# Layer 1's stacks in DRAM: each pair's 2 KB with a gap of 16 bytes behind it

## The chip, the core and the metric

The kernel runs on one core of a Trainium2 chip. The metric is the device time of one execution in microseconds (us). It is given as the median of several runs, and as the time of one execution that the hardware profiler recorded. The core's engines are TensorE (PE), VectorE (DVE), ScalarE (ACT), GpSimd (POOL) and SyncE (SP). SP does no arithmetic here: it issues nearly all of the DMA transfers, one after the other, and waits before each for what the transfer needs.

## The reference

The model is a decoder of two layers over x of 32 sequences x 128 tokens x 128 channels. Layer 0 has an RWKV block, two attentions with feed-forward, and a mixture of experts. Layer 1 has a self-attention with rotary positions, a cross-attention with SiLU in place of softmax, and a mixture of experts with capacity. A layer norm follows each. The change concerns the scores of layer 1's two attentions:

```python
# _L1_attn_ref: 16 heads of 8 channels
q = _rope(split_heads(x @ Wq + bq)); k = _rope(split_heads(x @ Wk + bk))
scores = jnp.einsum('bhqd,bhkd->bhqk', q, k) / np.sqrt(D_K)
probs = jax.nn.softmax(scores, axis=-1)
# _L1_xattn_ref: 16 heads of 8 channels
scores = jnp.einsum('bhqd,bhkd->bhqk', q, k) * SCALE
attn = jax.nn.silu(jnp.where(mask == 0, NEG_INF, scores))
```

## The kernel before

The work is cut into 8 groups of 4 sequences (G = 4, GT = 512 tokens). Each layer's part of a group is a list of units, each with a place on a common time line. `pipeline` (L1467) sorts all of them by place and runs them in that order, so that several groups and layers are under way at once. The tile framework then fixes each engine's own order and sets the semaphores. A tile of SBUF comes from a ring of a few buffers (`BUFS`, L35): the stacks are of the kind `big`, with five buffers of 8 KB in each partition, shared with other work.

In layer 1 a head has only 8 channels, and q and k are kept to nearly single precision by splitting each into three bf16 parts (`parts3`, L801, on GpSimd). The score is the sum of six products of parts. The kernel does that sum in one matmul: it puts the six parts of q that are wanted, 8 rows each, on 48 partitions, and the six parts of k that go with them in the same partitions. Such an arrangement is a stack. As the parts lie on the wrong partitions for it (128 partitions: channel, parity of the head and number of the pair of heads), they go through DRAM:

- `scratch` (L810) makes three tensors `d_st` in DRAM, used in turn, of 64 rows x 2 parities x 8 pairs x 2 (q and k) x 512 tokens in bf16. One row, parity and pair has 2 KB, q and k beside each other; one row of both parities has 32 KB. Rows 48 to 63 are filled once from the input `pad_bf` (L816), near the start of the program.
- `spill` (L824) writes one group's parts. L829 writes the three parts to the rows 0 to 23, in pieces of 2 KB; L831 (once for q, once for k) the rows 24 to 39, in pieces of 1 KB; L832 the rows 40 to 47, in pieces of 1 KB. SP issues all four. They can start as the parts are done on GpSimd.
- `stack` (L835) reads half of the pairs back, once for each parity, into the partitions 0 to n and 64 to 64 + n (L843). Four consecutive pairs of one row are contiguous in DRAM: 8 KB. n is 50 in the self-attention, where rows 48 and 49 carry the maximum of the scores (written into the stack later, by `mwrite`, L1011, and `mread`, L1016, through the small DRAM tensor `d_m`), and 48 in the cross-attention. Each group has four reads in each attention, 64 in all.

`cross` (L979) and `probs` (L1130) run the matmuls on the stacks. On SP's queue the transfers around these are the loads and stores of x between layers (L217, L226), of the context (L580), of masks (L1117) and of expert weights (L1252); a transfer that has to wait holds all behind it.

Of the kernel before, what the change touches and what calls it, by code (L numbers as in the profile page):

```python
# [11 lines left out]
BF = mybir.dt.bfloat16  # L12
# [7 lines left out]

G = 4
GT = G * 128

# [47 lines left out]
class Net:  # L73
    def __init__(self, ctx, tc, a, ngroups):
# [15 lines left out]
        nc.gpsimd.tensor_copy(self.identb, self.ident)  # L90
        self.mhalf = self.cst.tile([128, G], F32, name="mhalf")
        nc.gpsimd.memset(self.mhalf, -0.5)
# [14 lines left out]
    def tok(self, tag):  # L107
        return self.t(tag, [G, 128])

# [93 lines left out]
    def half_turns(self, pts, es):  # L203

        calls = []
        for h in range(2):
            for b in range(G):
                for z in range(2):
                    r = slice(z * 64, z * 64 + 64)
                    calls.append((pts[z][:, (h * G + b) * 64:(h * G + b) * 64 + 64], es[h][r, b * 128:(b + 1) * 128],  # L210
                                  self.ident[r, r], None))
# [8 lines left out]
    def putx(self, g, x, final=False, queue=None):  # L220
        if final:
            d = self.a["out"][g * G:(g + 1) * G].rearrange("b s d -> s b d")
        else:
# [586 lines left out]
    def scratch(self, k):  # L810

        if self.dst is None:
            self.dst = []
            for i in range(3):
                d = self.dp.tile([64, 2, 8, 2, GT], BF, name=f"d_st{i}")
                self.nc.sync.dma_start(out=d[48:64], in_=self.a["pad_bf"])  # L816
                self.dst.append(d)
        return self.dst[k % 3]

# [4 lines left out]
    def spill(self, k, p):  # L824

        dma = self.nc.sync.dma_start
        d = self.scratch(k)
        rows = lambda lo, n: d[lo * 8:(lo + n) * 8].rearrange("(a d) r q z t -> (d r q) a z t", d=8)
        dma(out=rows(0, 3), in_=p)  # L829
        for z in range(2):  # L830
            dma(out=rows(3, 2)[:, :, z, :], in_=p[:, z:z + 2, z, :])  # L831
        dma(out=rows(5, 1)[:, 0], in_=p.rearrange("p a z t -> p (a z) t")[:, 0:6:5, :])  # L832
        return d

    def stack(self, d, h, n, slab=False):  # L835

        if slab:
            s = self.wp.tile([128, 4128], BF, name="w8", tag="w8", bufs=W8)
            s = s[:, 0:8 * GT].rearrange("p (q z t) -> p q z t", q=4, z=2)
        else:  # L840
            s = self.t("stack", [4, 2, GT], BF)
        for par in range(2):
            self.nc.sync.dma_start(out=s[par * 64:par * 64 + n], in_=d[0:n, par, h * 4:h * 4 + 4])  # L843
        return s

    def pad9(self):
# [92 lines left out]
    def att_units(self, g, getw, done):  # L939
# [129 lines left out]
        for j in range(8):  # L1069
            h = j // 4  # L1070
            u = [(L6["smax"], lambda j=j: smax(j)), (L6["probs"], lambda j=j: probs(j), 2),
                 (L6["values"], lambda j=j: values(j), 1)]
            if j == 0:
                u += [(0, load), (L6["pre"], pre), (L6["spill"], spill)]
                u += [(L6["v"] + 2 * b, lambda b=b: vproj(b)) for b in range(G)]
                for i in range(2):
                    u += [(L6["rope"] + 4 * i, lambda i=i: rope(i, 0)), (L6["rope"] + 2 + 4 * i, lambda i=i: rope(i, 1)),
                          (L6["part"] + 4 * i, lambda i=i: part(i))]
            if j % 4 == 0:
                u.append((L6["take"], lambda h=h: take(h)))  # L1080
            if j % 4 == 3:
                m = L6["mrow"]
                u += [(m, lambda h=h: mrow(h)), (m + 2, lambda h=h: mwrite(h)), (m + L6["mread"], lambda h=h: mread(h))]
            if h:
                u.append((L6["norm"], lambda b=j % 4: norm(b)))
            if j == 5:
                u += [(L6["norm"] - 2, again), (L6["norm"], bias)]
            if j == 7:
                o = L6["oproj"]
                u += [(o, oproj), (L6["done"], lambda: done(st["ln"](), nc.scalar))]  # L1090
            units.append([p if len(p) > 2 else (*p, -p[0]) for p in u])
# [13 lines left out]
    def xat_units(self, g, getw, done):  # L1105
# [103 lines left out]
        for j in range(8):  # L1209
            u = [(L7["probs"], lambda j=j: probs(j), 2), (L7["values"], lambda j=j: values(j), 1)]  # L1210
            if j == 0:
                u += [(0, load), (L7["pre"], pre), (L7["spill"], spill), (L7["mask"] - 2, mload), (L7["mask"], mask)]
                u += [(L7["v"] + b, lambda b=b: vproj(b)) for b in range(G)]
                for i in range(2):
                    u += [(L7["one"] + 2 * i, lambda i=i: one(i, *((st["kh"], st["kl"]) if i else (st["xh"], st["xl"])))),
                          (L7["part"] + 2 * i, lambda i=i: part(i))]
                u += [(t, lambda h=h: take(h)) for h, t in enumerate(L7["take"])]
            if j % 2:
                u.append((L7["oproj"], lambda b=j // 2: oproj(b)))
            if j == 7:  # L1220
                u += [(L7["ln"], lambda: st.update(y=st["ln"]())), (L7["done"], lambda: done(st["y"]))]
            units.append([p if len(p) > 2 else (*p, -p[0]) for p in u])
# [425 lines left out]
```

## Time and profile before

| | us |
|---|---|
| median of 3 runs (lowest, highest) | 1808.09 (1808.03, 1809.1) |
| the profiled execution | 1817.27 |
| its span, first to last instruction | 1815.5 |
| PE busy, share of the span | 1628.6, 90% |
| DVE busy | 1380.2, 76% |
| ACT busy | 1214.1, 67% |
| POOL busy | 982.6, 54% |
| stack reads L843, first and last issue | 1130.2, 1520.3 |

The granted clock of TensorE was 0.961 of full speed over the span. The page's slices are 40 equal parts of the span, some 45.4 us each; a digit is a busy share in tenths. "DMA" is the mean busy share of the core's 16 DMA engines. A DMA engine counts as busy while a packet of its own is under way, also if the packet waits somewhere. The chain of waits goes back from the last instruction, at each step to what released it. A wait of SP ("SPq") is time in which its queue stood still.

In the profile's list of transfers, each of the 32 reads of 50 rows moves 400 KB and each of the 32 reads of 48 rows 384 KB. A group's spill is three transfers of 256 KB and one of 768 KB. The three pad writes move 512 KB each.

### The profile page before, as it was taken

What the parts mean: (1) busy time and instruction counts of PE and PEld (TensorE: products, weight loads), DVE (VectorE), ACT (ScalarE), POOL (GpSimd) and SP (SyncE); (2) the same over time, 40 slices, a digit from 0 to 9 for tenths busy, and PEclk for the clock granted to TensorE, in tenths of its full rate; (3) what the DMA queues carried; (4) which work ended last, traced back from release to release, by engine and by line L of the source; (5) the groups of instructions that cost most, each with busy time, mean ns of one, the idle gap of its engine ahead of it and who ended that gap; (6) DMA issues with size and microseconds to landing.
All of it is one profiled execution on the core that took longest, in us unless ns stands there. A gap on an engine that the chain in (4) does not pass through costs nothing.

```text
span 1815.5 us, 45617 instructions
## 1 busy us (share of the span) xinstructions
PE 1628.6 (90%) x15858; PEld 1311.8 (72%) x15858; DVE 1380.2 (76%) x5303; ACT 1214.1 (67%) x3889; POOL 982.6 (54%) x1324
## 2 busy tenths in 40 slices
PE   4898898899999999998899999998877887989898
PEld 2676676777777777776688888876655554778898
DVE  7879888887777777775676667778864775788896
ACT  3786777878888888887744554336666666656654
POOL 4657676777665555564534444345533443446455
PEclk7899999999999999999999999999989998899999
DMA  6100110111110000000123443336667987223222
GB/s 172 36 26 23 41 44 24 33 48 56 49 39 9 27 25 26 27 25 14 58 79 124 167 154 109 108 124 196 182 184 173 246 231 204 93 71 105 82 94 70
DMA packets 86214, 163.43 MB, mean 90 GB/s; under 512 B 12968, under 2 KB 34352, under 8 KB 80368
## 3 DMA queue, kind: packets, MB, share of 16 engines
q1 hardware_dynamic: 83248, 146.89, 27.5%
q0 software_dynamic: 1584, 11.54, 1.5%
q8 instruction: 125, 2.05, 0.5%
q10 hardware_dynamic: 1152, 2.10, 0.3%
q14 instruction: 105, 0.86, 0.2%
HBM read 106.75 MB, written 55.31 MB: 89 GB/s over the span
## 4 chain that ended last, share of the span: by engine, by line
PE 41%; DVE 20%; ACT 15%; POOL 11%; issue 6%; DMA 6%; SPq 1%; POOLq 0%; ACTq 0%; DVEq 0%
ACT e L483 8%; PE mm L157 5%; PE S L771 5%; PE PV L169 4%; PE mm L158 4%; PE mm L159 4%; DVE e L478 4%; PE S L169 3%; POOL x L255 3%; PE mm L541 3%; PE PT L1395 3%; POOL e L487 2%; DMA x<-x 2%; DVE x L263 2%; PE S L620 1%
## 5 line engine op out<-in xcount | busy, mean ns | idle before, releaser
L483 ACT ACTIVATE e<-e,nm 128x128 f32<-128x128 f32 x1024 | 398.8, 394 | 111.8 <-POOL nm L480 111.8
L487 POOL TENSOR_TENSOR e<-e,ri 128x512 f32<-128x512 f32 x256 | 268.4, 1054 | 175.2 <-DVE ri L485 146.2
L478 DVE CUSTOM_DVE_ANT_0 e<-S,msk 128x128 f32<-128x128 f32 x1024 | 227.9, 284 | 12.0 <-PE PT L168 9.1
L483 ACT ACTIVATION_READ_ACCUMULATOR e<-e,nm 128x1 f32 x1024 | 196.2, 192 | 0.0
L169 PEld LDWEIGHTS S<-qk 64*128 64x128 f32 x2048 | 128.3, 190 | 78.0 <-issue 40.6
L169 PE MATMUL S<-qk 64*128 64x128 f32 x2048 | 151.3, 287 | 30.2 <-DVE pt L501 16.3
L169 PE MATMUL PV<-pt,v 128*64 128x128 f32 x2048 | 141.9, 281 | 10.8 <-DVE big L523 10.6
L157 PE MATMUL mm<-xs,w 128*128 128x512 f32 x296 | 130.9, 446 | 16.5 <-ACT xs L150 5.0
L276 POOL TENSOR_SCALAR rsqv<-bmv 128x4 f32<-128x4 f32 (+1 forms) x73 | 22.5, 308 | 215.3 <-DVE bmv L243 179.9
L771 PEld LDWEIGHTS S<-w,v 128*128 128x128 f32 x1024 | 129.1, 191 | 10.2 <-ACT v L760 1.9
L760 ACT ACTIVATE v<-mm,col_moe_b 128x512 f32<-128x512 f32 x128 | 85.6, 686 | 75.4 <-PE mm L159 74.8
L771 PE MATMUL S<-w,v 128*128 128x128 f32 x1024 | 133.9, 276 | 1.7 <-ACT v L760 1.7
L485 DVE RECIPROCAL ri<-su 128x4 f32<-128x4 f32 x256 | 43.6, 172 | 120.7 <-ACT e L483 90.7
L169 PEld LDWEIGHTS PV<-pt,v 128*64 128x64 f32 x2048 | 110.9, 138 | 21.6 <-issue 6.7
L158 PE MATMUL mm<-xs,w 128*128 128x512 f32 x296 | 119.8, 405 | 1.6 <-DVE xs L151 1.4
L159 PE MATMUL mm<-xs,w 128*128 128x512 f32 x296 | 119.1, 402 | 0.0
L169 PE MATMUL PV<-e,w 128*32 128x128 f32 (+1 forms) x2048 | 90.3, 299 | 26.3 <-ACT e L1027 13.9
L501 DVE COPY pt<-PT 128x256 f32<-128x256 f32 x256 | 97.3, 415 | 8.4 <-ACT pt L501 7.6
L523 DVE TENSOR_TENSOR big<-PV,big 128x512 fp32r<-128x512 f32 x128 | 87.3, 682 | 19.5 <-ACT big L522 19.0
L1000 DVE TENSOR_REDUCE amx<-mm 128x4 f32<-128x512 f32 x128 | 82.1, 684 | 24.3 <-PE mm L169 24.2
L501 ACT COPY pt<-PT 128x256 f32<-128x256 f32 x256 | 81.8, 373 | 25.2 <-PE PT L168 25.0
L541 PE MATMUL mm<-big 128*128 128x512 f32 x384 | 96.9, 398 | 0.0
(326 smaller groups left out, 4803.7 us busy)
## 6 DMA issues: line engine op xcount, KB each, us to landing
x<-x SPq DMA_DIRECT2D x151, 256.0 KB
pt<-d_w SPq DMA_DIRECT2D x64, 256.0 KB
big<-d_st SPq DMA_DIRECT2D x32, 400.0 KB
d_st<-qk SPq DMA_DIRECT2D x48, 256.0 KB
d_st<-qk SPq DMA_DIRECT2D x16, 768.0 KB
big<-d_st SPq DMA_DIRECT2D x32, 384.0 KB
d_w<-big POOLq DMA_DIRECT2D x11, 1024.0 KB, 6.4
w<-d_w SPq DMA_DIRECT2D x7, 1024.0 KB
```

The source lines that it names most:

```text
L157: mm(out=out, lhsT=wh, rhs=xh, start=True, stop=False)
L158: mm(out=out, lhsT=wh, rhs=xl, start=False, stop=False)
L159: mm(out=out, lhsT=wl, rhs=xh, start=False, stop=True)
L169: return self.nc.tensor.matmul(out=out, lhsT=lhsT, rhs=rhs, **more)
L478: self.seen = nc.vector.tensor_tensor_reduce(e[:, t], s[h][:, t], msk[:, t], 1.0, NEG, ALU.add, ALU.max, mx[:, b:b + 1])
L483: nc.scalar.activation(e[:, t], e[:, t], AF.Exp, bias=nm[:, b:b + 1], scale=0.125, accum_out=su[:, b:b + 1])
L487: i = nc.gpsimd.tensor_tensor(e3, e3, ri.unsqueeze(2).to_broadcast([128, G, 128]), ALU.mult)
L501: last = (nc.vector.tensor_copy if h else nc.scalar.copy)(d, s_)
L523: nc.vector.tensor_tensor(lo, o, hi.bitcast(F32), ALU.subtract)
L541: nc.tensor.matmul(out=out, lhsT=a_, rhs=b_, start=n == 0, stop=n == 3 * PER - 1)
L760: nc.scalar.activation(h, hp, AF.Gelu, bias=w["b1"][:, k:k + 1])
L771: nc.tensor.matmul(out=o[:, b, :], lhsT=hs[i][:, b * 128:(b + 1) * 128], rhs=w["w2"][:, k * 128:k * 128 + 128], start=i == 0, stop=i == 1)
```

## The change

`d_st` gets 16 bytes (GAP = 8 elements of bf16) behind each pair's 2 KB. A pair then takes 2,064 bytes and a row of 16 pairs 33,024. All that write or read it leave the gap out. What lay contiguous over several pairs is now a row of separate pieces: a stack read has four pieces of 2 KB for each row instead of one of 8 KB, and a pad write 256 pieces of 2 KB instead of 16 rows of 32 KB. The pieces of `spill` keep their sizes; their addresses in DRAM move. Inside SBUF nothing moves.

```diff
+GAP = 8
 G = 4
 GT = G * 128
...
-                d = self.dp.tile([64, 2, 8, 2, GT], BF, name=f"d_st{i}")
-                self.nc.sync.dma_start(out=d[48:64], in_=self.a["pad_bf"])
+                d = self.dp.tile([64, 2, 8, 2 * GT + GAP], BF, name=f"d_st{i}")
+                self.nc.sync.dma_start(out=d[48:64, :, :, 0:2 * GT], in_=self.a["pad_bf"].rearrange("p r q z t -> p r q (z t)"))
...
-        rows = lambda lo, n: d[lo * 8:(lo + n) * 8].rearrange("(a d) r q z t -> (d r q) a z t", d=8)
-        dma(out=rows(0, 3), in_=p)
+        rows = lambda lo, n: d[lo * 8:(lo + n) * 8].rearrange("(a d) r q x -> (d r q) a x", d=8)
+        dma(out=rows(0, 3)[:, :, 0:2 * GT], in_=p.rearrange("p a z t -> p a (z t)"))
         for z in range(2):
-            dma(out=rows(3, 2)[:, :, z, :], in_=p[:, z:z + 2, z, :])
-        dma(out=rows(5, 1)[:, 0], in_=p.rearrange("p a z t -> p (a z) t")[:, 0:6:5, :])
+            dma(out=rows(3, 2)[:, :, z * GT:(z + 1) * GT], in_=p[:, z:z + 2, z, :])
+        dma(out=rows(5, 1)[:, 0, 0:2 * GT].rearrange("p (z t) -> p z t", z=2), in_=p.rearrange("p a z t -> p (a z) t")[:, 0:6:5, :])
...
-            self.nc.sync.dma_start(out=s[par * 64:par * 64 + n], in_=d[0:n, par, h * 4:h * 4 + 4])
+            self.nc.sync.dma_start(out=s[par * 64:par * 64 + n].rearrange("p q z t -> p q (z t)"),
+                                   in_=d[0:n, par, h * 4:h * 4 + 4, 0:2 * GT])
```

## The prediction

> **What bounds the kernel now.** I read the page first, for the stages. Layer 1's two attentions, the only ones that use the stacks, lie between 1109 and 1565 us.
>
> ```profile
> PE   4898898899999999998899999998877887989898
> DMA  6100110111110000000123443336667987223222
> GB/s 172 36 26 23 41 44 24 33 48 56 49 39 9 27 25 26 27 25 14 58 79 124 167 154 109 108 124 196 182 184 173 246 231 204 93 71 105 82 94 70
> ```
>
> TensorE is the busiest engine in almost every slice. Only in slices 27 to 34 (1225 to 1565 us) do the DMA engines come near it, at six to nine tenths. The change can matter there, and at the start (the pad writes). Next, stretches in which one group's stacks are read with little beside them, and one spill:
>
> ```profile
> core 0: us, PE busy (x) PEld busy (x) DVE busy (x) ACT busy (x) POOL busy (x), PEclk, DMA share, GB/s
> 1127.20:1129.40 2.20, 2.20 (x19) 1.99 (x18) 0.00 (x0) 0.99 (x2) 0.00 (x0) 1.00 0.96 357
> 1131.00:1141.50 10.50, 10.50 (x74) 9.57 (x73) 10.11 (x47) 3.89 (x7) 2.42 (x26) 1.00 0.59 157
> 1439.90:1450.10 10.20, 7.97 (x114) 5.34 (x114) 7.96 (x23) 6.30 (x13) 8.49 (x9) 0.88 1.02 187
> ```
>
> The second last column is the busy share of the 16 DMA engines. The spill (first row) moves 357 GB/s with all engines. Four reads of 50 rows (second row) keep 0.59 x 16 = 9.4 engines busy and move 157, that is 16.6 GB/s for a busy engine instead of 23.2; four reads of 48 rows (third row) keep all 16 busy and move 187, other traffic included. So a stack read is slow while its engines count as busy. The packet records say the same: an 8 KB packet of other loads takes 309 ns, one of a 50-row read 489 on average (1131 to 1141 us), one of a 48-row read 720 (1440 to 1450 us). Packets of 2 KB take 84 ns nearly everywhere, 86 to 91 in spills; 1 KB 46, 512 B 27.
>
> Then the chain of waits over 1090 to 1570 us, its DMA pieces alone, and what holds SP:
>
> ```profile
> 1301.42 7.11 DMA d_m<-m
> 1309.16 2.89 DMA x<-x
> 1320.19 7.86 DMA big<-d_st
> 1365.82 6.35 DMA d_m<-m
> 1372.78 4.59 DMA big<-d_st
> 1391.76 6.26 DMA big<-d_st
> 1500.35 9.36 DMA x<-x
> 1530.85 2.57 DMA x<-x
> ```
>
> ```profile
> SPq L1019 <- DMA d_m<-m: 62.9, 15, 6.9
> SPq L843 <- DMA d_st<-qk: 49.7, 18, 8.0
> ```
>
> Start, length, what. Stack reads end the wait three times, for 7.86 + 4.59 + 6.26 = 18.7 us; small transfers queued behind stacks and spills on the same queue five times, for 28.3 us. Together 47 us of the path are DMA time that the change touches. Elsewhere in the 480 us the chain runs over TensorE, VectorE and ScalarE, and the reads are hidden under them: under TensorE busy all 10.50 us in the second row above, for example. L843 waits 49.7 us in total for its spill to land, and all later SP transfers wait behind it.
>
> **The change part by part.** In the built program, TensorE, VectorE, ScalarE and GpSimd have the same instructions in the same order, and SP the same transfers in the same order. Only shapes differ: L843 from 50x4096 to 50x4x1024 elements, L832 from 256x1x512 to 128x2x512, L816 from 16x16384 to 256x1024. No wait is added.
>
> *Reads (L843, 64 of them).* Each 8 KB piece becomes four of 2 KB, on the same engines and to the same partitions. From packets without contention: 4 x 84 = 336 against 309 ns, 27 more. A 50-row read puts 5 rows on each of 10 engines, a group of four reads 20 packets in a row: 20 x 27 = 0.54 us more. A 48-row group has 12 in a row on 16 engines: 0.32 us. These are upper bounds of about 5% (0.54 of 10.4) and 3%. The lower bound is nothing: where packets already wait 180 (489 - 309) or 411 ns (720 - 309) for something shared, one engine's gap of 7 ns is another's turn. The long packets are nearest to that, so I take 1.5%: 0.7 us of the 47 us on the path (bounds 0 and 2.4). A gain is the first rival below.
>
> What is shared is not in a row. [...]
>
> *Writes (L829, L831, L832, three a group at 1 KB and one at 2 KB pieces).* Same bytes; the pieces now start at multiples of 16 bytes with 2,064 between them. A group's spill takes about 2.2 us (first row above) for L829 and 16 packets x 46 ns = 0.74 us for each of the other three, 4.4 us in all. The nearest row of transfers off their boundary are the shifted loads L324 and L325 at the start: 508 B packets take 27 ns, as 512 B ones do, so the lower bound is nothing; but they read DRAM, and none here writes it off a boundary. A near upper bound treats each piece as two: 2 x 46 = 92 against 84, and 2 x 27 = 54 against 46, 8 ns each; (24 + 48) x 8 ns = 0.58 us a group. Of that the last two transfers, (24 + 16) x 8 = 0.32 us, hold L843. With six exposed groups (the eight waits of the chain, of which the first two belong together, and the fourth and fifth) that is 1.9 us; I take a third, 0.6, since the shifted row says nothing and the doubled row 10%. The far bound is the pad writes: 1.2 us for a 32 KB packet alone, up to 3.1 in the crowd, 2.6 times; it is the second rival.
>
> [...]
>
> *Issue and pads.* L843 takes 330 ns to issue now; L829 with its three dimensions takes 371. Only the first of four delays what follows: 0.04 us x 6 = 0.2. L832 should fall from 519 to L831's 382, but it stands before GpSimd's next part, which SP waits for anyway (L831 for L807: 39.0 us in all): nothing; without that cover, 16 x 0.14 = 2.2 us gained. The pads become 48 packets of 2 KB an engine, 48 x 84 = 4.0 us, against 31.4 to 38.2 us now; the next loads are issued at 41.0. Nothing, with 2.8 us to spare.
>
> Sum: 0.7 + 0.6 + 0.2 = 1.5 us. The profiled execution (span 1815.5, 1817.27 with what lies around it) would become 1817.0 and 1818.8; against the median of the runs, 1808.09, it is 1809.6. The forecast's own range is 0 to +4.5 (2.4 + 1.9 + 0.2, all bounds high).
>
> **The rivals.**
>
> *Reads become quicker (faster).* If a packet is long because it is long, and not for what it shares, all 2 KB pieces take 84 ns: a 50-row group 20 x 336 = 6.7 us instead of 10.4, a 48-row one 12 x 336 = 4.0 instead of 9.5. For it: 2 KB packets took 84 to 91 ns in the very stages where 8 KB ones took 700. Against: those go to or from all 128 partitions, and 8 KB packets to 128 partitions (the expert weights, 1570 us on) also take 309. It would save some 40% of the 18.7 us and a quarter of the 28.3, 14.6 us; as TensorE and VectorE are busy 80% of these stretches and take over half of the waits, about 7: 1801.
>
> *Writes off their boundary are slow (slower).* Place: the spill, whose landing L843 waits for, with d_m, x and the masks queued behind it on SP. At 1.6 times their time, midway to the far bound, a group's 4.4 us become 7.0; five exposed groups at 2.6 us are 13 us: 1821. At the far bound, 35 us. It passes the limit of what can be told at 3.6 / 5 = 0.7 us a group, writes 16% slower. For it: SP does wait there, 49.7 us. Against: writes run at 357 GB/s with packets only 2 to 7 ns over the floor of 84. The pads would then also reach past 41.0 us, where a load of xT is on the chain.
>
> *It doesn't do what it says.* The engine could still be given 8 KB on the SBUF side, which stays contiguous. Then reads cost the same and the writes' share stays: 1808.7.
>
> **How the numbers follow.** What a measurement of this kernel can tell from no change is about 0.2%, 3.6 us. Forecast 0.48, of which 0.36 within 3.6 us and 0.12 above; quick reads 0.21, all faster; slow writes 0.27, all slower; unchanged pieces 0.04, within. So faster 0.21, same 0.40, slower 0.39. The likeliest gives 1809.6. With cases of both signs, the range runs from 1800, which cuts off the larger half of quick reads (0.1), to 1823, which cuts off the slow writes beyond 15 us (0.1); the forecast's own is 1808 to 1812.6.
>
> **What would show it.** Packets of 2 KB to big from d_st, four times as many, and a 50-row group of 10.4 to 10.9 us with a share near 0.6: right. A group below 8 us: quick reads. A spill (L829) above 2.6 us, and L843 waiting well over 49.7 us for d_st: slow writes. I would be wrong in kind if the time moves while groups and spills keep their lengths: then the order of arrivals, not their cost, decides.

## The result, and the profile after

The changed kernel takes 1817.39 us (median of 7 runs, 1811.88 to 1823.46), the kernel before 1808.22 (7 runs, 1806.58 to 1815.25): 1.0041 of before, 95% interval 1.0024 to 1.0058, or 4 to 11 us more. The profiled execution took 1818.77 us, with a span of 1817.0. In single profiles the loss shows in layer 1's stage alone: from the issue of the first L829 to that of the last (the sixteenth) before took 383.9 us, after 392.7. The part ahead of it, layer 0, was 4 us shorter (first L829 at 1122.2 us instead of 1126.3), so the spans of the two profiles differ by less than the medians. The odd one is the profile of before: that execution lies 9 us above its kernel's median, and in the profiles of all the variants below the first L829 comes at 1118 to 1122 us.

The stretches of after that answer to those shown of before, one spill and one group of reads of either kind (columns as there; second last is the busy share of the DMA engines):

```profile
1123.00:1125.50 2.50, 2.50 (x23) 2.29 (x21) 0.00 (x0) 1.12 (x2) 0.00 (x0) 1.00 0.84 315
1126.90:1137.10 10.20, 10.20 (x71) 9.27 (x70) 9.81 (x46) 3.56 (x8) 2.41 (x26) 1.00 0.62 161
1440.90:1451.40 10.50, 8.25 (x118) 5.45 (x117) 8.61 (x23) 6.41 (x14) 8.79 (x9) 0.91 1.03 181
```

All reads are in pieces of 2 KB now: the page counts 96,342 DMA packets instead of 86,214, which is three more for each of 3,136 rows that are read and 720 more for the pads. A group of 50-row reads still takes 10.2 us and one of 48-row reads 10.5, against 10.4 and 10.2. The 2 KB packets of a spill with little beside it still take 86 to 88 ns (the window here is 0.3 us wider than the one of before, hence the lower rate). Neither the reads became quicker nor does a quiet spill look slower.

What changed is who waits. SP's waits, and the DMA pieces of the chain over 1090 to 1570 us (line numbers from 1 higher on; L844 was L843, L1021 L1019):

```profile
SPq L1021 <- DMA d_m<-m: 71.4, 15, 7.8
SPq L844 <- DMA d_st<-qk: 59.6, 19, 10.2
```

```profile
1244.90 4.65 DMA big<-d_m
1255.17 7.30 DMA d_st<-qk
1277.93 7.11 DMA d_st<-qk
1302.12 8.80 DMA d_m<-m
1311.54 2.79 DMA x<-x
1388.02 3.52 DMA d_st<-qk
1391.99 6.62 DMA big<-d_st
1413.07 6.19 DMA big<-d_st
1461.84 11.82 DMA x<-x
1504.26 10.18 DMA x<-x
```

The wait of the stack reads for their spill has grown from 49.7 to 59.6 us, that for the small `d_m` tensors behind it from 62.9 to 71.4. The chain's DMA pieces are 69 us instead of 47, and three of them are now spills that have not landed (7.30, 7.11, 3.52 us), which before ended no wait of the chain. So the suspicion falls on the writes, although their packets look the same: what is late is their landing, the moment when the transfer reports that it is done.

### The profile page after: what moved, and what is told of

Read it like the earlier page. It is cut to its first block, busy times and chain, and to the rows that moved or that the text cites. A ratio compares the mean times of both kernels' runs of the same rounds, so it can differ in the third digit from the quotient of the medians.

```text
span 1817.0 us, 45617 instructions
## 1 busy us (share of the span) xinstructions
PE 1626.8 (90%) x15858; PEld 1308.8 (72%) x15858; DVE 1376.1 (76%) x5303; ACT 1214.0 (67%) x3889; POOL 983.3 (54%) x1324
## 2 busy tenths in 40 slices
DMA packets 96342, 163.43 MB, mean 90 GB/s; under 512 B 12968, under 2 KB 34352, under 8 KB 93680
## 4 chain that ended last, share of the span: by engine, by line
PE 42%; DVE 18%; ACT 14%; POOL 12%; DMA 7%; issue 6%; SPq 1%; POOLq 0%; ACTq 0%; DVEq 0%
ACT e L484 7%; PE S L772 5%; PE mm L158 5%; PE PV L170 4%; PE mm L159 4%; PE mm L160 4%; DVE e L479 4%; PE S L170 3%; POOL x L256 3%; PE PT L1397 3%; POOL e L488 3%; PE mm L542 3%; DMA x<-x 2%; DVE x L264 1%; PE S L621 1%
## 5 line engine op out<-in xcount | busy, mean ns | idle before, releaser
L772 PEld LDWEIGHTS S<-w,v 128*128 128x128 f32 x1024 | 130.5, 193 | 10.5 <-ACT v L761 2.2
L1002 DVE TENSOR_REDUCE amx<-mm 128x4 f32<-128x512 f32 x128 | 82.1, 683 | 31.3 <-PE mm L170 31.2
```

The lines of the kernel that those rows point to most:

```text
L772: nc.tensor.matmul(out=o[:, b, :], lhsT=hs[i][:, b * 128:(b + 1) * 128], rhs=w["w2"][:, k * 128:k * 128 + 128], start=i == 0, stop=i == 1)
```

## The experiments

Three theories were to be told apart: *pieces* (more and smaller reads), *address* (transfers off a boundary; later split into reads and writes), *order* (chance of arrivals). In all the variants of this kernel but the last one, the compute engines have the instructions of before in the same order. Ratios are against before, measured beside it on the same chip, with 95% intervals. "Stage" is the time from the first L829 to the sixteenth, 383.9 us before and 392.7 after, and "wait for spills" the wait of the stack reads for d_st, 49.7 and 59.6 us; both come from one profile of each kernel.

**A gap of 256 bytes.** `GAP = 128`.

> The gap is 256 bytes instead of 16: as many pieces of 2 KB, but every piece starts at a multiple of 256 bytes again. Theory 'pieces' (four times as many pieces make a stack read longer, wherever they start): as the changed kernel, 1.004 of before, 1814 to 1818 us. Theory 'address' (pieces off a boundary are slow, in reads or in spills): as before, 1.000, some 1808 to 1810 us. Theory 'order' (no transfer is longer, arrivals only shift by chance): anything between 0.998 and 1.004, without a longer group of reads.

Measured: 1.0010 (0.9996 to 1.0024). As many pieces of 2 KB, and an interval that ends where the change's begins; stage 382.6 us, wait for spills 50.5 us. Pieces is not the main cause. This profile also tells which signs to trust: its chain has three spills too (6.59, 6.86 and 3.33 us, in 45.0 us of DMA pieces), and its wait for `d_m` is 67.9 us, all without a loss that can be told. The wait for spills is the better sign.

**No gap, 16 bytes off.**

```diff
-                d = self.dp.tile([64, 2, 8, 2, GT], BF, name=f"d_st{i}")
+                d = self.dp.tile([64 * 32 * GT + 8], BF, name=f"d_st{i}")
+                d = d[8:64 * 32 * GT + 8].rearrange("(n r q z t) -> n r q z t", r=2, q=8, z=2, t=GT)
```

> The layout of before, without gaps, but each of the three DRAM tensors begins 16 bytes later: reads in pieces of 8 KB, all pieces of reads, spills and pads 16 bytes off a boundary. Pieces: 1.000 of before. Address: 1.004, with groups of 48-row reads of 10.2 us instead of 9.5.

Measured: 1.0041 (1.0023 to 1.0058), stage 394.2 us, wait 64.7 us. With reads of 8 KB as before, the address alone gives a loss as large as the change's. The reads are issued in their old form here, so the loss doesn't need the dearer issue of the changed reads either (374 ns each in the median, against 330).

**The gap in one attention only.** Six tensors, `GAPS = (8, 0)` or `(0, 8)`, `self.dst[k // 8 * 3 + k % 3]`.

> Six DRAM tensors, three for each attention; only those of the self-attention (50-row reads) have the 16 byte gap, those of the cross-attention are as before. By the two profiles the changed kernel loses some 5 us of its 9 between 1230 and 1280 us, in the self-attention, and 4 us between 1490 and 1515 us, in the cross-attention. If these are costs of the reads there: 1.002 to 1.003. If only 48-row reads get longer (10.2 instead of 9.5 us a group, where 50-row ones stay at 10.3): 1.000 to 1.001.

> The counterpart of e3_att: six DRAM tensors, only those of the cross-attention have the 16 byte gap. The self-attention alone cost 1.0016 of before. If the price is that of the off-boundary writes, paid in both attentions, the rest is here: 1.002 to 1.003, with L843's wait for spills longer in the last eight groups alone. If the self-attention carried all: 1.000 to 1.001.

Measured: self-attention alone 1.0016 (1.0002 to 1.0029), cross-attention alone 1.0026 (1.0007 to 1.0044). The two add up to 1.0042, as much as the change. The cross-attention pays: the wait for spills is 53.8 us, and the increase stands in its groups (27.8 us there instead of 23.9, in the self-attention's 26.0 instead of 25.8). For the self-attention it is hardly shown: the interval almost reaches 1, and the wait is 50.8 us, 26.9 in its own groups. Six tensors instead of three are a change of their own, and no run has them without a gap.

**The transfers alone.** A kernel of DMAs only, run once, with each group of four reads by itself, four times:

```python
for h in range(2):
    for par in range(2):
        dma(out=t[par * 64:par * 64 + n, h * 4:h * 4 + 4], in_=d[0:n, par, h * 4:h * 4 + 4, 0:P2])
```

> Computes nothing of the model; it writes zeros and times the disputed transfers alone, each group of four reads (two halves, two parities) four times with nothing beside it. A: no gap, G: 16 byte gap, W: 256 byte gap, O: no gap, 16 bytes off; f: 50 rows, e: 48 rows. P and Q are one tensor of 128 rows read into all 128 partitions, without and with a gap. Pieces: G and W alike and longer than A and O, by 0.3 to 0.6 us a group. Address: G and O alike and longer than A and W. Sharing on the SBUF side: P moves 1 MB for each half in 8 x 309 ns = 2.5 us, 5 us for both, against 9.5 to 10.3 us for four reads into 48 or 50 partitions; Q some 8 x 336 x 2 = 5.4 us. If long packets were the reason, G and W would be far shorter than A (6.7 against 10.3 us). Writes of 2 KB pieces (2 MB): some 6 us in A, and the same in G and O unless an off-boundary write costs.

VectorE's waits for each kind: in total, times, longest (four groups each; A, G, W, O, P, f and e as in the expectation; P's longest holds the write of its tensor too):

```profile
DVE z L53 <- DMA rGf<-dG: 47.8, 8, 9.9
DVE z L53 <- DMA rWf<-dW: 46.9, 8, 9.8
DVE z L53 <- DMA rAf<-dA: 46.3, 8, 9.8
DVE z L53 <- DMA rOf<-dO: 45.8, 8, 9.9
...
DVE z L53 <- DMA rAe<-dA: 44.9, 8, 9.8
DVE z L53 <- DMA rGe<-dG: 44.3, 8, 9.6
...
DVE z L70 <- DMA rP<-dP: 37.0, 4, 14.0
```

Reads of 50 rows take 46.3 us without and 47.8 with the gap, 0.4 us a group more, and 46.9 with 256 bytes; reads of 48 rows 44.9, 44.3 and 45.5. Neither the number of pieces nor their boundary matters much when they are alone. P, 28 to 33% more bytes (128 rows for 100 or 96) into all 128 partitions, is quicker than any of them: its packets span 6.1 to 6.3 us a group, against 9.2 to 10.3 in A, and their median is 309 ns. That the long packets wait on the SBUF side is the author's estimate from these spans; it isn't shown by itself, since P differs in two more things, in the distance of its rows in DRAM (the gaps change that too, without such an effect) and in having two transfers for four, which was not tried by itself. The same read with the gap, Q, takes 0.3 us a group more than P (waits of 39.4 and 37.0 us in all; without the longest, which holds the write, 23.8 and 23.0 for three groups).

This run also gave the first sign of the writes: the packets of a write of 2 MB in pieces of 2 KB span 6.0 us in A, 5.6 in G and W, and 7.1 to 7.4 in O, off the boundary without a gap.

**Reads off, or writes off.** The layout of before, with two views of each tensor 16 bytes apart; the scores are of shifted tokens.

```diff
-                d = self.dp.tile([64, 2, 8, 2, GT], BF, name=f"d_st{i}")
+                d = self.dp.tile([64 * 32 * GT + 256], BF, name=f"d_st{i}")
+                self.dread.append(d[136:136 + 63 * 32 * GT].rearrange("(n r q z t) -> n r q z t", r=2, q=8, z=2, t=GT))
+                d = d[128:128 + 64 * 32 * GT].rearrange("(n r q z t) -> n r q z t", r=2, q=8, z=2, t=GT)
...
-        return d
+        return self.dread[k % 3]
```

This is reads off: written from element 128 on, read from 136 on. In writes off the two are 120 and 128.

> The layout of before; spills and pads write at boundaries of 256 bytes, but the reads (8 KB pieces) start 16 bytes later, so that the scores are taken of tokens shifted by eight. Theory 'reads' (an off-boundary read is what costs): 1.003 to 1.004 of before. Theory 'writes' (off-boundary writes to DRAM cost): 1.000, and the stage from the first to the last spill 383 us, L843's waits for spills some 50 us.

> The counterpart: spills and pads write 16 bytes before a boundary of 256, reads start at the boundary, so that the scores are again taken of tokens shifted by eight. Writes: 1.004 of before, stage 393 us, L843's waits 60 to 65 us. Reads: 1.000.

Measured: reads off 0.9999 (0.9981 to 1.0017), writes off 1.0062 (1.0043 to 1.0081, five runs). The waits for spills, of the 256 byte gap, of reads off and of writes off:

```profile
SPq L844 <- DMA d_st<-qk: 50.5, 19, 8.1
SPq L845 <- DMA d_st<-qk: 48.3, 18, 7.5
SPq L845 <- DMA d_st<-qk: 60.9, 19, 7.5
```

The stage of writes off is 393.2 us, as expected; that of reads off is 387.0, not the 383 expected, in an execution 6 us above its kernel's median. These two runs settle the cause: reads (of 8 KB pieces) 16 bytes off cost nothing that can be told (0.9999), writes to DRAM 16 bytes off do (1.0062). The pads are off their boundary too in writes off, but the first L829 comes at 1121.5 us, and in reads off at 1121.9, so nothing is lost at the start.

**The spill alone, and behind reads.** The four writes of a spill in two kernels of DMAs only, each run once, in several layouts.

> Computes nothing of the model; it writes no output and times a spill's transfers alone: w the three-part write in 2 KB pieces, q one write of 1 KB halves, b the one that writes both halves, qbkw all four in the kernel's order, and mf and me a spill issued right behind four reads of 50 or 48 rows of another tensor. Layouts: A none, G 16, H 64, W 256 bytes of gap, O no gap and 16 bytes off; four times each. In the first such run writes of 2 KB pieces with a gap of 16 bytes were no slower than aligned ones (5.6 us for 2 MB), those without a gap and 16 bytes off were (7.1). Writes: b and q are longer in G and O than in A, W and H, since there two pieces meet inside a line, by 0.2 us or more; qbkw by 0.5 us or more in G, more in O; mf and me as much. Reads: all alike, but me longer in G and O.

> Computes nothing of the model and writes no output: the spill's transfers alone, four times for each layout. Without gap: A on the boundary, B 16, C 32, D 64, E 128 bytes off; G, H, J with gaps of 16, 32 and 64 bytes. Four spills took 31.3 us with A and J (64 bytes), 34.7 with G, 39.1 with B in the run before. Meeting within 32 bytes: C, D, E and H 31 to 32 us. Within 64 bytes: C some 39, H some 34, D and E 31 to 32. Every start off 256 bytes: C, D, E alike, some 39.

VectorE's waits for a small read-back behind each spill, with four spills of each layout and nothing beside them, in the second of these runs (A on the boundary, B, C, D, E 16, 32, 64, 128 bytes off without a gap; G, H, J gaps of 16, 32, 64):

```profile
DVE z L49 <- DMA bqbkwB<-dB: 37.2, 4, 9.6
DVE z L49 <- DMA bqbkwG<-dG: 33.5, 4, 9.0
DVE z L49 <- DMA bqbkwC<-dC: 32.2, 4, 8.4
DVE z L49 <- DMA bqbkwH<-dH: 32.0, 4, 8.0
DVE z L49 <- DMA bqbkwD<-dD: 31.8, 4, 8.0
DVE z L49 <- DMA bqbkwE<-dE: 31.6, 4, 8.0
DVE z L49 <- DMA bqbkwA<-dA: 31.4, 4, 7.9
```

16 bytes off costs 1.5 us a spill, (37.2 - 31.4) / 4; the 16 byte gap 0.5, and 0.8 in the run before it (34.7 against 31.3). 32 bytes or more cost 0.2 or less. So alone, the price was paid in the two layouts in which written pieces meet inside the same 32 bytes: all do in B; in G only the q and k halves of every second pair do, since 16 bytes lie between the pairs. The expectation had this as one of its three answers. The three-part write L829 alone, whose pieces all have the gap behind them, costs nothing in G (21.7 against 21.9), though half of them start off 32 bytes. The price needn't show in the packets that meet. L832 alone, in pieces of 1 KB, lands 1.1 us later in B (22.0 against 17.5 for four), while its packets take 47 to 49 ns on average in B as in A. In the whole spill it is the 2 KB packets of L829, issued behind the 1 KB ones, that are long: up to 613 ns in B and 742 in G, in the others no more than 152. G's four spills differ much: the one with the 742 ns lands at 9.0 us, the others at 8.0 to 8.3, those of A at 7.8 to 7.9.

Behind four reads of 48 rows (first of the two runs; here H is the 64 byte gap and O is 16 bytes off), VectorE waits for the reads (re) and then for what remains of the spill (bme):

```profile
DVE z L81 <- DMA reG<-eG: 29.6, 4, 7.7
DVE z L81 <- DMA reH<-eH: 28.5, 4, 7.3
DVE z L81 <- DMA reA<-eA: 28.4, 4, 7.3
DVE z L81 <- DMA reW<-eW: 27.9, 4, 7.8
...
DVE z L49 <- DMA bmeO<-dO: 30.9, 4, 8.1
...
DVE z L49 <- DMA bmeG<-dG: 24.6, 4, 6.6
...
DVE z L49 <- DMA bmeH<-dH: 24.3, 4, 6.2
...
DVE z L49 <- DMA bmeW<-dW: 22.3, 4, 5.7
DVE z L49 <- DMA bmeA<-dA: 22.0, 4, 5.7
```

When the spill has landed is told by the sum of both waits: 50.4 us in A, 50.2 in W, 52.8 in H, 54.2 in G. So beside these reads the gap of 16 bytes costs 0.95 us a spill, (54.2 - 50.4) / 4, and 64 bytes, free when alone (31.3 us for four spills, as in A), cost 0.6; 256 bytes cost nothing to speak of (50.2). Behind 50-row reads the sums are 55.3 (G), 53.4 (H) and 53.3 (W): 16 bytes cost 0.5 us more than 256, and 64 bytes no more.

**64 bytes of gap, and 32 bytes off, in the kernel.**

> The gap is 64 bytes: pieces start at multiples of 64, not of 256. If the price is paid for parts of a 64 byte line that two pieces share or that a write fills only in part, there are none left: 1.000 to 1.001, as with a gap of 256 bytes. [...]

> As the run in which the DRAM tensors begin 16 bytes off (1.0041 of before), but 32 bytes off: no gap, reads of 8 KB, two written pieces still meet inside a line of 64 bytes, but no longer inside one of 32. If the price of the writes is paid where two pieces meet within 32 bytes: 1.000. If the line is of 64 bytes or more, or if every start off 256 bytes costs: 1.004.

Measured: gap of 64 bytes 1.0027 (1.0012 to 1.0043), stage 387.0, wait 57.6 us; 32 bytes off 1.0023 (1.0008 to 1.0038), stage 389.1, wait 55.2 us. Both expectations of no loss (1.000 to 1.001, and 1.000) fall; the change's own loss, 1.0041, lies inside the first interval and just outside of the second. In the kernel's traffic, these writes, whose pieces start at multiples of 64 or at 32 bytes past a multiple of 256, lose time although no two meet inside 32 bytes: by the ratios a half to two thirds of the change's loss, but the intervals overlap. For 64 bytes the waits behind 48-row reads show the same (0.6 us a spill), those behind 50-row reads don't (53.4 and 53.3 us).

**A quicker kernel.** As one read into all 128 partitions was quickest (6.1 to 6.3 us a group), the parity was put outermost in the tensors; each of the four writes becomes two, of every second partition (the pads and part of the code are left out here).

```diff
+                d = self.dp.tile([2, 64, 8, 2 * GT], BF, name=f"d_st{i}")
...
+        for r in range(2):
+            rows = lambda lo, n: d[r, lo * 8:(lo + n) * 8].rearrange("(a d) q x -> (d q) a x", d=8)
+            pr = p[r:128:2]
...
+        self.nc.sync.dma_start(out=s.rearrange("p q z t -> p q (z t)"),
+                               in_=d.rearrange("r n q x -> (r n) q x")[:, h * 4:h * 4 + 4])
...
+    order = np.array([(2 * q + r) * 8 + k for k in range(8) for q in range(8) for r in range(2)])
```

> A try at a quicker kernel, from what the reads alone showed: DRAM tensors with the parity outermost, so that one read fills all 128 partitions (64 rows of each parity, the pad rows too, 1 MB) instead of two of 50 or 48 rows; no gap, all pieces on boundaries. Each write of the spill is two of 64 partitions, every second one. Theory 'sharing on the SBUF side': a group's reads take 6.3 us as in the run of the transfers alone, instead of 9.5 to 10.4; of the 47 us of the chain that are DMA time some 10 go: 0.993 to 0.997 of before. If the eight smaller writes or the new order cost as much: 1.000. If reads are bound by DRAM after all: slower than before by the 25% more bytes, 1.002 to 1.005.

Measured: 0.9960 (0.9945 to 0.9975), 1800.92 us. It beats both kernels. A group's reads:

```profile
1122.90:1128.90 6.00, 6.00 (x42) 5.42 (x41) 5.72 (x30) 2.43 (x5) 2.41 (x26) 1.00 0.91 350
```

6.0 us instead of 10.4, at 350 GB/s instead of 157, with 8 KB packets of 309 ns in the median; the DMA pieces of its chain over 1090 to 1570 us sum to 24.6 us instead of 47, and the wait for spills is 36.4 us. As the writes and the engines' order changed with the reads, the run doesn't divide the gain between them.

## Why the prediction was right or wrong

*The sum and its sign.* 1809.6 us was forecast, 1.5 more than before; measured are 9.2 more by the medians and 7.4 by the ratio. Slower was right. The time lies in the range of 1800 to 1823 only because that range had been drawn to hold the rivals too; the forecast's own ended at 1812.6. What came is the second rival, at six to seven tenths of its price of 13 us: the likeliest case was the wrong one.

*Reads.* 0.7 us was taken, between 0 and 2.4. Alone, 50-row groups got 0.4 us longer and 48-row ones not at all; with the 256 byte gap, which keeps the pieces and takes the address away, the kernel loses 1.8 us (-0.7 to 4.3). That agrees with the term; the runs can't tell it from nothing. The reason given, that an engine's gap is filled by others that wait for the same thing, isn't shown, nor what they would wait for. A wait on the SBUF side, the author's estimate, agrees with the quick read over all 128 partitions (6.1 to 6.3 us a group instead of 9.2 to 10.3); but there, where an 8 KB packet takes 309 ns in the median, the gap costs 0.3 us a group, no more than the 0.4 of the 50-row reads.

*Writes: the step that failed.* The term was 0.6 us: a third of 0.32 us, in six exposed groups. Measured, a spill of the changed layout lands 0.5 to 0.85 us later alone and 0.5 to 0.95 behind reads, and the stack reads' wait for spills grew by 9.9 us over the sixteen groups, 0.6 each on average (not evenly: that of one group went from 5.9 to 10.2). Three things in the term are wrong. The price was put near the lower bound because shifted loads take 27 ns as aligned ones do; those are reads, and in the kernel reads 16 bytes off cost nothing that can be told (0.9999) while writes 16 bytes off do (1.0062). It was worked out as longer packets, while what grew was the time to landing: a quiet spill's packets take 86 to 88 ns in both kernels. And it was charged to six groups only, those where the chain of before had a DMA wait, the delay in all others being taken as hidden. How many groups do pay isn't shown: 7.4 us at 0.5 to 0.95 us each would be eight to fifteen, an estimate, and the chain of one profile doesn't tell, since three spills stand in that of the 256 byte gap as well, without a loss. The rival had the place right (the landing that L843 waits for, and what stands behind it on SP), but not the size: 2.6 us in each of five groups, where some 0.6 in each of sixteen was measured.

*Where to look for it.* I wrote that a spill above 2.6 us would show slow writes. It didn't: the quiet L829 looks as before, as it does alone, where its own pieces don't meet. The other sign, L843's wait well over 49.7 us, did. I had also written that I would be wrong in kind, with the order of arrivals deciding, if the time moved while groups and spills kept their lengths. By the windows that is what came, and the sign misled: a landing can be late without longer packets (16 bytes off, L832 alone landed 1.1 us later, its packets at 47 to 49 ns as on the boundary), and the variants show that the address of the writes decides (1.0062 with the writes off, 0.9999 with the reads).

*Quick reads.* This rival fell, as its argument against had it: groups of 10.2 and 10.5 us. (Its 9.5 us for a 48-row group before is not the row shown, which has 10.2; the quiet ones span 9.3 to 10.2.)

*Issue and pads.* L832's issue fell from 519 to 382 ns and L843's rose from 330 to 374, as said; L832 alone, with its new form, became quicker by 0.3 us a spill with gaps of 32 or 64 bytes (16.3 and 16.5 against 17.5 for four). Nothing shows at the start: the loads after the pads are issued at 41.1 us instead of 41.0.

*That it doesn't do what it says.* It does: packets below 8 KB rose from 80,368 to 93,680, which is four for each of the 3,136 rows that are read and 768 for the pads, all of 2 KB.

Still open: why writes 32 or 64 bytes off a multiple of 256 lose time in the kernel's traffic (1.0023 and 1.0027) and cost 0.2 us a spill or less alone, how the 1.0041 of the 16 byte gap divides between halves that meet inside 32 bytes and starts off 256, and how much the pieces cost, between nothing and 0.2%. Between 1.0023 and 1.0062 neighbouring intervals overlap, so the order of these losses isn't shown.

## What to carry to other kernels

Padding a DRAM scratch tensor by a few bytes moves most of the later writes off the multiples of 256 bytes at which they started. Here gaps of 16 and 64 bytes cost time (1.0041 and 1.0027), as did a start 16 or 32 bytes later (1.0041 and 1.0023); a gap of 256 bytes cost nothing that can be told (1.0010, 0.9996 to 1.0024), and 128 was not tried in the kernel. Of these paddings, 256 bytes or none is the choice; and look at when writes land, not at how long their packets take. A read can be slow while its engines count as busy: here cutting four reads of 50 rows into smaller pieces left them at 10.2 us, from 10.4, and the kernel with one read over all 128 partitions took 6.0 us a group, with 28 to 33% more bytes (its writes and the engines' order changed too). When a price is paid by every transfer of a kind, don't charge it only to the waits on the chain of one profile: the total wait for these transfers is the better guide, and the chain changes from variant to variant.

## What the runs showed of the hardware that was not expected

Writes whose pieces meet inside 32 bytes of DRAM landed later: with nothing beside them a spill 16 bytes off took 1.5 us more than the 7.85 of one on the boundary, while the same layout 32, 64 or 128 bytes off took 0.2 more or less. The delay needn't show in the packets of the pieces that meet (L832 alone: 47 to 49 ns with it and without); in the whole spill the 2 KB packets of the write behind them took up to 742 ns, against no more than 152 in the layouts without the delay. In the kernel's traffic a start 32 bytes off and a gap of 64 cost time too (1.0023 and 1.0027), reads 16 bytes off nothing that can be told (0.9999). Four reads of 50 rows alone, cut into 800 packets, took nearly as long as in 200 (47.8 and 46.3 us for four groups): the mean packet was 127 to 130 ns long, where one of 2 KB takes 84 in the median when it goes to all 128 partitions.
